# Transposed squares ordered by target quadrant, and diagonal chunk pairs computed on and above the diagonal only

## The chip, the core and the metric

The kernel runs on one core of a Trainium2 chip. Its metric is the device time of one execution in microseconds (us). The kernel before takes 1891.2 us, the median of three runs (1889.86 to 1892.12). The profiled execution took 1890.13 us, of which the profile covers a span of 1888.3 us.

A core has a matrix engine (TensorE, PE in the profile; its loads of stationary weights are PEld), a vector engine (VectorE, DVE), an engine for activation functions (ScalarE, ACT), a general engine (GpSimd, POOL) and a queue that here does nothing but issue transfers (SyncE, SP). Every engine runs its own instructions in the order in which the built program holds them.

## The reference, cut to what matters

The input has four images. Layer 0 turns each into a matrix `q` of 128 channels by 4096 positions and lets its 4096 positions attend to each other:

```python
q = xs.reshape(B, C * R * R, hw)                 # here C*R*R = 128 rows, hw = 4096
energy = jnp.einsum('bci,bcj->bij', q, q)        # 4096 x 4096, symmetric
d = jnp.sqrt(jnp.diagonal(energy, axis1=1, axis2=2))
energy = energy / (d[:, :, None] * d[:, None, :])
attn = jax.nn.softmax(energy, axis=-1)
out = jnp.einsum('bcj,bij->bci', q, attn)
out = gamma * out + xs
```

Layer 1 takes each image as 4096 tokens of 128 features (32 blocks of 128 rows in the kernel), normalises them, adds a linear attention, and then a mixture of eight experts of which the two likeliest are used for each token.

What matters here is that the normalised energy is symmetric, so exp(energy) is too. A square of exp(energy) above the diagonal serves twice: as it is, and transposed.

## The kernel before

The 4096 positions are eight chunks of 512 columns (`NCH = 8`, `CH = 512`), each of four blocks of 128 (`NJ = 4`). For each image, `attend` walks over chunk pairs (i, jc) with jc <= i: 36 pairs, 28 of them with jc < i (off the diagonal), 8 with jc = i (on it). One pair has four steps, one for each 128-row block j. A step computes a 128x512 strip of energy (`pe`), its exponential (`pr`), and the product of the strip with the values, summed up in `po` for chunk i.

```python
for i in range(NCH):
    po = ps_o.tile([P, CH], F32, tag="po", ...)
    def values(pend, i=i, po=po):
        pr, t = pend
        nc.tensor.matmul(po, qT[t // NJ][:, t % NJ, :], pr, start=(t == 0), stop=(t == NJ * (i + 1) - 1))
    for jc in range(i + 1):
        off = jc < i
        if off:
            F = fpool.tile([P, CH // S, NJ, S], F32, tag="F", ...)          # S = 32, fpool: 2 buffers
        for j in range(NJ):
            t = NJ * jc + j
            pe = ps_e.tile([P, CH], F32, tag="pe", ...)                     # 2 buffers
            nc.tensor.matmul(pe, qn[jc][:, ts(j, P)], qn[i], start=True, stop=True)
            pr = ppool.tile([P, CH], F32, tag="pr", ...)                    # 6 buffers
            nc.scalar.activation(pr, pe, AF.Exp, accum_out=sums[:, t, i : i + 1])
            if pend is not None:
                values(pend)
            if off:
                nc.vector.transpose(F[:, :, j, :], pr)                      # 32x32 blocks
            pend = (pr, t)
            ...                                # one step of an older pair's transposed share, if it is due
        if off:
            G = gpool.tile([P, NJ, 4, P], F32, tag="G", ...)                # 3 buffers
            blocks = F.rearrange("p (ib q) j c -> p q ib (j c)", q=4)
            for a in range(4):
                for q in range(4):
                    nc.sync.dma_start(G[ts(q, S), :, a, :], blocks[ts(a, S), q])
            late.append((clock[0] + LAG, transposed_share(b, st, i, jc, G)))
    values(pend)
    o = opool.tile([P, CH], F32, tag="o", ...)
    nc.vector.tensor_copy(o, po)
```

VectorE's transpose works within blocks of 32x32. To make a whole transpose of a square, the blocks must also move between groups of 32 partitions; that is what the 16 transfers from `F` to `G` do, one for each pair of source and target group. The transposed square is then used a little later, four matmuls and four row sums for each pair:

```python
def transposed_share(b, st, i, jc, G):
    pg = ps_g.tile([P, CH], F32, tag="pg", ...)                             # 1 buffer
    for ib in range(NJ):
        nc.tensor.matmul(pg, st["qT"][i][:, ib, :], G[:, ib].rearrange("p a j -> p (a j)"),
                         start=(ib == 0), stop=(ib == NJ - 1))
        junk = work.tile([P, CH], BF16, tag="junk", ...)
        nc.scalar.activation(junk, G[:, ib]..., AF.Copy, accum_out=st["sums"][:, NJ * i + ib, jc : jc + 1])
        if ib == NJ - 1:
            o = st["o"][jc]...
            nc.vector.tensor_tensor(o, o, pg..., ALU.add)
        yield ...
```

Beside the steps of `attend`, two other streams of work are woven in. `prep` loads a part of the next image and makes `qT` (the values) and `qn` (the normalised columns):

```python
def prep(b, kc, st):
    load_tokens(xx, b, 8 * kc, 8)                       # transfers issued by SyncE
    for g in range(2):
        pt = psum_t(f"ptq_{b}_{kc}_{g}")                # TensorE transposes, 2 buffers in all for psum_t
        ...
        nc.vector.tensor_copy(qT..., pt...)
    for s in range(2):
        nc.vector.tensor_tensor(sq, qT[:, s], qT[:, s], ALU.mult)
        nc.vector.tensor_reduce(ss[:, ts(s, NJ)], sq, AX.X, ALU.add)
    pow_neg_half(rn[:, :, 0], ss)                       # GpSimd
    for s in range(2):
        nc.vector.tensor_tensor(qs, qT[:, s], rn..., ALU.mult)
        pt = psum_t(f"ptn_{b}_{kc}_{s}")                # TensorE transposes
        ...
        nc.scalar.activation(qn, pt, AF.Copy)
```

And `layer1` does layer 1 of the image before. In it, `pat` is the attention's matmul, then row statistics on VectorE (`bs_f`, `dm_f`), a power on GpSimd (`rsf`), a normalisation on ScalarE (`xg`), transposes on TensorE (`ptf`), and the experts' matmuls (`py`, with `pbe` for their bias after a transpose `ptg` of the gates). After the last image `layer1` runs alone: this is the tail. The order of instructions on every engine is fixed when the kernel is built; it need not be the order of the source.

Of the kernel before, what the change touches and what calls it, by code (L numbers as in the profile page):

```python
# [9 lines left out]
F32 = mybir.dt.float32  # L10
BF16 = mybir.dt.bfloat16
AF = mybir.ActivationFunctionType
ALU = mybir.AluOpType
# [5 lines left out]
def kernel(  # L19
# [10 lines left out]
    expert_b: bass.AP,  # L30
    out: bass.AP,
):

# [18 lines left out]
    nc = tc.nc  # L54
    P = 128
    B, C, H, W = x.shape
    N = (H // 2) * (W // 2)
    NB = N // P
    CH = 512
    NCH = N // CH  # L60
    NJ = CH // P
    HW2 = W // 2
    KT = 32
    S = 32
# [10 lines left out]
    fpool = ctx.enter_context(tc.tile_pool(name="fpool", bufs=2))  # L75
    gpool = ctx.enter_context(tc.tile_pool(name="gpool", bufs=3))
    work = ctx.enter_context(tc.tile_pool(name="work", bufs=2))
    stat = ctx.enter_context(tc.tile_pool(name="stat", bufs=2))
# [123 lines left out]

    def transposed_share(b, st, i, jc, G):

        pg = ps_g.tile([P, CH], F32, tag="pg", name=f"pg_{b}_{i}_{jc}")
        for ib in range(NJ):
            nc.tensor.matmul(  # L207
                pg, st["qT"][i][:, ib, :], G[:, ib].rearrange("p a j -> p (a j)"),
                start=(ib == 0), stop=(ib == NJ - 1),
            )  # L210
            junk = work.tile([P, CH], BF16, tag="junk", name=f"junk_{b}_{i}_{jc}_{ib}")
            nc.scalar.activation(  # L212
                junk, G[:, ib].rearrange("p a j -> p (a j)"), AF.Copy,
                accum_out=st["sums"][:, NJ * i + ib, jc : jc + 1],
            )
            if ib == NJ - 1:
                o = st["o"][jc].rearrange("p (j a c) -> p a j c", a=4, c=S)
                nc.vector.tensor_tensor(o, o, pg.rearrange("p (a j c) -> p a j c", a=4, c=S), ALU.add)  # L218
            yield "done" if ib == NJ - 1 else None

    def attend(b, st):

        qT, qn = st.setdefault("qT", {}), st.setdefault("qn", {})
        st["sums"] = sums = stat.tile([P, NB, NCH], F32, tag="sums", name=f"sums_{b}")
        st["o"] = []

        for i in range(NCH):
            po = ps_o.tile([P, CH], F32, tag="po", name=f"po_{b}_{i}")
            pend = None

            def values(pend, i=i, po=po):
                pr, t = pend
                nc.tensor.matmul(po, qT[t // NJ][:, t % NJ, :], pr, start=(t == 0), stop=(t == NJ * (i + 1) - 1))  # L233

            for jc in range(i + 1):
                off = jc < i
                if off:
                    F = fpool.tile([P, CH // S, NJ, S], F32, tag="F", name=f"F_{b}_{i}_{jc}")
                for j in range(NJ):
                    t = NJ * jc + j  # L240
                    pe = ps_e.tile([P, CH], F32, tag="pe", name=f"pe_{b}_{i}_{t}")
                    nc.tensor.matmul(pe, qn[jc][:, ts(j, P)], qn[i], start=True, stop=True)  # L242
                    pr = ppool.tile([P, CH], F32, tag="pr", name=f"pr_{b}_{i}_{t}")
                    nc.scalar.activation(pr, pe, AF.Exp, accum_out=sums[:, t, i : i + 1])  # L244
                    if pend is not None:
                        values(pend)
                    if off:
                        nc.vector.transpose(F[:, :, j, :], pr)  # L248
                    pend = (pr, t)
                    clock[0] += 1  # L250
                    if late and late[0][0] <= clock[0]:
                        if next(late[0][1], "done") == "done":
                            late.pop(0)
                    yield
                if off:
                    G = gpool.tile([P, NJ, 4, P], F32, tag="G", name=f"G_{b}_{i}_{jc}")
                    blocks = F.rearrange("p (ib q) j c -> p q ib (j c)", q=4)
                    for a in range(4):
                        for q in range(4):
                            nc.sync.dma_start(G[ts(q, S), :, a, :], blocks[ts(a, S), q])  # L260
                    late.append((clock[0] + LAG, transposed_share(b, st, i, jc, G)))
            values(pend)
            o = opool.tile([P, CH], F32, tag="o", name=f"o_{b}_{i}")
            nc.vector.tensor_copy(o, po)
            st["o"].append(o)
# [7 lines left out]
    def layer1(b, st, alone):  # L273
# [79 lines left out]
        def transpose_rows(g):  # L353
# [3 lines left out]
            if alone:  # L357
                if g % 4 == 0:
                    keep["G"] = gpool.tile([P, 4, 4, P], F32, tag="G", name=f"xnT_{b}_{g}")
                xnT = keep["G"][:, g % 4].rearrange("p j t -> p (j t)")  # L360
# [198 lines left out]
    for b in range(B):  # L559
        streams = []  # L560
        if b == 0:
            for kc, begin, end in ((1, 0, 8), (2, 10, 26), (3, 30, 60)):
                streams.append((prep(0, kc, states[0]), begin, end, 9))
            streams.append((setup_weights(), 60, 70, 3))
        else:
            p = states[b - 1]
            work_left = layer1(b - 1, p, False)
            streams.append((work_left, 9, 138, SIDE))
        if b + 1 < B:
            for kc, at in enumerate((96, 121, 128, 134)):  # L570
                streams.append((prep(b + 1, kc, states[b + 1]), at, at + 9, 9))
        done = [0] * len(streams)
        for t, _ in enumerate(attend(b, states[b])):
            for n, (steps, begin, end, count) in enumerate(streams):
                while t >= begin and done[n] * (end - begin) < (t + 1 - begin) * count:
                    next(steps, None)
                    done[n] += 1
        for steps, *_ in streams:
            for _ in steps:
                pass  # L580
    finish_late()
    last = states[B - 1]
# [40 lines left out]
```

## Time and profile before

| | before |
|---|---|
| time, median of three | 1891.2 us |
| span of the profile | 1888.3 us |
| TensorE busy | 1815.8 us (96%), 5090 matmuls |
| VectorE busy | 900.1 us (48%) |
| ScalarE busy | 957.7 us (51%) |
| GpSimd busy | 292.6 us (15%) |
| `F` to `G` transfers | 1792 of 64 KB, median 2.0 us from issue to landing |
| transfer engines busy with the SyncE queue's packets | 32.4% |

A matmul on 32-bit data is two instructions in the profile, each with a weight load; a TensorE transpose is one. The mean duration of a matmul in the list of groups (595 ns for 512 columns) holds the way through the array, which overlaps with the next one; the distance from one start to the next is shorter and is read from the chain of work in order of time. Idle time of an engine is listed with what ended it. Where the list says "issue", nothing that the profile shows was waited for.

The tail begins about 1743 us after the start of the span.

### The profile page before, as it was taken

What the parts mean: (1) busy time and instruction counts of PE and PEld (TensorE: products, weight loads), DVE (VectorE), ACT (ScalarE), POOL (GpSimd) and SP (SyncE); (2) the same over time, 40 slices, a digit from 0 to 9 for tenths busy, and PEclk for the clock granted to TensorE, in tenths of its full rate; (3) what the DMA queues carried; (4) which work ended last, traced back from release to release, by engine and by line L of the source; (5) the groups of instructions that cost most, each with busy time, mean ns of one, the idle gap of its engine ahead of it and who ended that gap; (6) DMA issues with size and microseconds to landing.
All of it is one profiled execution on the core that took longest, in us unless ns stands there. A gap on an engine that the chain in (4) does not pass through costs nothing.

```text
span 1888.3 us, 20141 instructions
## 1 busy us (share of the span) xinstructions
PE 1815.8 (96%) x5090; PEld 872.5 (46%) x5090; DVE 900.1 (48%) x2201; ACT 957.7 (51%) x2925; POOL 292.6 (15%) x275
## 2 busy tenths in 40 slices
PE   6999999999999999999999999999999999999588
PEld 3444444444554444444554444444455444444543
DVE  3343223345355454555455445563535544443676
ACT  2444444344556545554556545554545645544364
POOL 0000000003000121211200112221300022121336
PEclk9999999999999999999999999999999999999789
DMA  5333343431243233334233333333323323235001
GB/s 118 77 89 74 84 101 85 111 81 46 69 104 78 62 82 75 87 93 96 59 87 76 81 72 84 74 85 85 76 64 90 80 60 85 65 85 117 1 12 34
DMA packets 314274, 145.61 MB, mean 77 GB/s; under 512 B 32528, under 2 KB 314160, under 8 KB 314160
## 3 DMA queue, kind: packets, MB, share of 16 engines
q1 hardware_dynamic: 310528, 142.73, 32.4%
q10 hardware_dynamic: 3632, 1.60, 0.4%
q8 instruction: 42, 0.69, 0.2%
q14 instruction: 72, 0.59, 0.1%
HBM read 18.38 MB, written 8.39 MB: 14 GB/s over the span
## 4 chain that ended last, share of the span: by engine, by line
PE 87%; DVE 5%; POOL 3%; ACT 2%; SPq 1%; DMA 1%; issue 1%; ACTq 0%; POOLq 0%; DVEq 0%
PE po L233 24%; PE pe L242 24%; PE pg L207 20%; PE py L525 6%; PE py L532 5%; DVE df L342 1%; PE pbe L515 1%; PE pat L423 1%; SPq L260 1%; PE ptn L193 1%; POOL T L350 1%; ACT xn L325 1%; PE pgram L368 1%; POOL rsa L109 1%; PE ptx L356 1%; PE ptq L171 1%
## 5 line engine op out<-in xcount | busy, mean ns | idle before, releaser
L244 ACT ACTIVATE pr<-pe 128x512 f32<-128x512 f32 x576 | 343.9, 597 | 580.5 <-PE pe L242 580.1
L233 PE MATMUL po<-pr,qT 128*128 128x512 f32 x1152 | 590.3, 595 | 4.3 <-ACT pr L244 2.7
L248 DVE STREAM_TRANSPOSE F<-pr 128x512 f32<-128x512 f32 x448 | 311.4, 705 | 341.6 <-ACT pr L244 311.6
L242 PE MATMUL pe<-qn,qn 128*128 128x512 f32 x896 | 455.8, 593 | 0.2
L207 PE MATMUL pg<-G,qT 128*128 128x512 f32 x896 | 426.4, 598 | 2.8 <-DMA G<-F 2.8
L233 PEld LDWEIGHTS po<-pr,qT 128*128 128x128 f32 x1152 | 213.9, 190 | 272.1 <-issue 233.0
L212 ACT ACTIVATE junk<-G 128x512 bf16<-128x512 f32 x448 | 276.0, 623 | 4.9 <-DMA G<-F 4.9
L207 PEld LDWEIGHTS pg<-G,qT 128*128 128x128 f32 x896 | 171.0, 192 | 215.3 <-issue 209.3
L242 PEld LDWEIGHTS pe<-qn,qn 128*128 128x128 f32 x896 | 161.4, 190 | 161.1 <-issue 159.7
L534 ACT ACTIVATE tmp<-py,gate 128x128 f32<-128x128 f32 x512 | 145.7, 370 | 172.6 <-PE py L532 163.8
L527 DVE SCALAR_TENSOR_TENSOR acc<-py,gate,acc 128x128 f32<-128x128 f32 x512 | 174.9, 348 | 101.6 <-PE py L525 87.9
L218 DVE TENSOR_TENSOR o<-o,pg 128x512 f32<-128x512 f32 x112 | 76.8, 686 | 230.2 <-PE pg L207 228.9
L538 POOL TENSOR_TENSOR tmp<-tmp 128x512 f32<-128x512 f32 x64 | 81.3, 1271 | 559.2 <-ACT tmp L534 535.7
L532 PE MATMUL py<-ew_sb,xn 128*128 128x512 f32 x256 | 131.9, 601 | 4.1 <-ACT tmp L534 4.1
L242 PE MATMUL pe<-qn 128*128 128x512 f32 x256 | 131.0, 595 | 0.0
L525 PE MATMUL py<-ew_sb,xn 128*128 128x512 f32 x256 | 129.3, 592 | 0.0
L244 ACT ACTIVATION_READ_ACCUMULATOR pr<-pe 128x1 f32 x576 | 114.5, 199 | 0.0
L109 POOL TENSOR_TENSOR rn<-ss,neg_half 128x8 f32<-128x8 f32 x16 | 26.3, 1642 | 433.2 <-DVE ss L183 433.2
L212 ACT ACTIVATION_READ_ACCUMULATOR junk<-G 128x1 f32 x448 | 87.3, 195 | 0.0
L109 POOL TENSOR_TENSOR rsf<-dm_f,neg_half 128x8 f32<-128x8 f32 x16 | 26.3, 1644 | 359.2 <-DVE dm_f L320 359.2
L532 PEld LDWEIGHTS py<-ew_sb,xn 128*128 128x128 f32 x256 | 48.5, 192 | 65.1 <-issue 48.0
L525 PEld LDWEIGHTS py<-ew_sb,xn 128*128 128x128 f32 x256 | 48.0, 190 | 59.2 <-issue 39.4
(114 smaller groups left out, 1221.8 us busy)
## 6 DMA issues: line engine op xcount, KB each, us to landing
G<-F SPq DMA_DIRECT2D x1792, 64.0 KB, 2.0
xx<-in_x_dram SPq DMA_DIRECT2D x64, 128.0 KB, 3.0
T<-in_x_dram SPq DMA_DIRECT2D x16, 512.0 KB, 5.7
out_dram<-acc SPq DMA_DIRECT2D x128, 64.0 KB, 1.8
ew_sb<-in_L_ffn_expert_w_dram ACTq DMA_DIRECT2D x1, 512.0 KB, 5.5
raw_w<-in_L_attn_Wv_dram ACTq DMA_DIRECT2D x1, 512.0 KB
raw_w<-in_L_attn_Wk_dram ACTq DMA_DIRECT2D x1, 256.0 KB
raw_w<-in_L_attn_Wq_dram ACTq DMA_DIRECT2D x1, 256.0 KB
```

The lines of the kernel that those rows point to most:

```text
L207: nc.tensor.matmul(pg, st["qT"][i][:, ib, :], G[:, ib].rearrange("p a j -> p (a j)"), start=(ib == 0), stop=(ib == NJ - 1),)
L212: nc.scalar.activation(junk, G[:, ib].rearrange("p a j -> p (a j)"), AF.Copy, accum_out=st["sums"][:, NJ * i + ib, jc : jc + 1],)
L218: nc.vector.tensor_tensor(o, o, pg.rearrange("p (a j c) -> p a j c", a=4, c=S), ALU.add)
L233: nc.tensor.matmul(po, qT[t // NJ][:, t % NJ, :], pr, start=(t == 0), stop=(t == NJ * (i + 1) - 1))
L242: nc.tensor.matmul(pe, qn[jc][:, ts(j, P)], qn[i], start=True, stop=True)
L244: nc.scalar.activation(pr, pe, AF.Exp, accum_out=sums[:, t, i : i + 1])
L248: nc.vector.transpose(F[:, :, j, :], pr)
L525: nc.tensor.matmul(py, xn[:, k, :], ew_sb[:, 0:4, :], start=True, stop=True)
L527: nc.vector.scalar_tensor_tensor(acc[:, j, :], py[:, ts(e, D)], gate[:, k, e : e + 1], acc[:, j, :], ALU.mult, ALU.add)
L532: nc.tensor.matmul(py, xn[:, k, :], ew_sb[:, 4:8, :], start=True, stop=True)
L534: nc.scalar.activation(tmp[:, jk, e, :], py[:, ts(e, D)], AF.Copy, scale=gate[:, k, 4 + e : 5 + e])
L538: nc.gpsimd.tensor_tensor(tmp[:, :, 0:2], tmp[:, :, 0:2], tmp[:, :, 2:4], ALU.add)
```

## The change

The change has two parts.

**The order within the transposed squares.** `F` and `G` get their quadrant as the outer dimension, so that each of the 16 transfers of a pair reads one run of 2 KB in each partition and writes one such run, instead of four runs of 512 bytes. The number of transfers for a pair and their bytes stay. The readers of `G` (the `pg` matmul and the row sum) then take four runs of 128 columns, 2 KB apart, where they took 512 columns in a row.

**The diagonal pairs.** A pair with jc = i is symmetric itself. Step j now computes only the columns from block j on (512, 384, 256 and 128 columns for `pe`, the exponential and `po`). What lies below the diagonal comes from the transposed share, which a diagonal pair now has too: three transposes, two clears of the part of `F` that is sent but not computed, 16 transfers of 48 KB, three `pg` matmuls and three row sums (384, 256 and 128 columns), and one addition. The last diagonal pair of the last image stays whole, so 31 of 32 pairs change. The row sums get one more column.

The diff, cut to its core:

```diff
     def transposed_share(b, st, i, jc, G):
         pg = ps_g.tile([P, CH], F32, tag="pg", name=f"pg_{b}_{i}_{jc}")
-        for ib in range(NJ):
-            nc.tensor.matmul(
-                pg, st["qT"][i][:, ib, :], G[:, ib].rearrange("p a j -> p (a j)"),
-                start=(ib == 0), stop=(ib == NJ - 1),
+        pgv = pg.rearrange("p (a f) -> p a f", a=4)
+        blocks = [(ib, P) for ib in range(NJ)] if jc < i else [(ib, S * ib) for ib in range(NJ - 1, 0, -1)]
+        for n, (ib, w) in enumerate(blocks):
+            last = n == len(blocks) - 1
+            src = G[:, :, ib, :w]
+            nc.tensor.matmul(pgv[:, :, :w], st["qT"][i][:, ib, :], src, start=(n == 0), stop=last)
             ... (the row sum and the addition follow in the same way)
-        st["sums"] = sums = stat.tile([P, NB, NCH], F32, tag="sums", name=f"sums_{b}")
+        st["sums"] = sums = stat.tile([P, NB, NCH + 1], F32, tag="sums", name=f"sums_{b}")
+        nc.gpsimd.memset(sums[:, :, NCH:], 0.0)
             ...
-                nc.tensor.matmul(po, qT[t // NJ][:, t % NJ, :], pr, start=(t == 0), stop=(t == NJ * (i + 1) - 1))
+                pr, t, c0 = pend
+                nc.tensor.matmul(
+                    po[:, c0:], qT[t // NJ][:, t % NJ, :], pr[:, c0:], start=(t == 0), stop=(t == NJ * (i + 1) - 1)
+                )
             for jc in range(i + 1):
-                off = jc < i
-                if off:
-                    F = fpool.tile([P, CH // S, NJ, S], F32, tag="F", name=f"F_{b}_{i}_{jc}")
+                within = jc == i
+                full = within and b == B - 1 and i == NCH - 1
+                if not full:
+                    F = fpool.tile([P, 4, NJ, NJ, S], F32, tag="F", name=f"F_{b}_{i}_{jc}")
+                    Fb = F.rearrange("p q ib j c -> p ib q j c")
                 for j in range(NJ):
-                    nc.tensor.matmul(pe, qn[jc][:, ts(j, P)], qn[i], start=True, stop=True)
+                    c0 = P * j if within and not full else 0
+                    nc.tensor.matmul(pe[:, c0:], qn[jc][:, ts(j, P)], qn[i][:, c0:], start=True, stop=True)
-                    nc.scalar.activation(pr, pe, AF.Exp, accum_out=sums[:, t, i : i + 1])
+                    nc.scalar.activation(pr[:, c0:], pe[:, c0:], AF.Exp, accum_out=sums[:, t, i : i + 1])
-                    if off:
-                        nc.vector.transpose(F[:, :, j, :], pr)
+                    if not within:
+                        nc.vector.transpose(Fb[:, :, :, j, :], pr)
+                    elif not full and j < NJ - 1:
+                        c1 = max(c0, P)
+                        nc.vector.transpose(Fb[:, c1 // P :, :, j, :], pr[:, c1:])
             ...
-                    G = gpool.tile([P, NJ, 4, P], F32, tag="G", name=f"G_{b}_{i}_{jc}")
-                    blocks = F.rearrange("p (ib q) j c -> p q ib (j c)", q=4)
+                    G = gpool.tile([P, 4, NJ, P], F32, tag="G", name=f"G_{b}_{i}_{jc}")
+                    ib0 = 0
+                    if within:
+                        nc.gpsimd.memset(F[:, :, 1, 2:, :], 0.0)
+                        nc.gpsimd.memset(F[:, :, 2:, 3, :], 0.0)
+                        ib0 = 1
+                    blocks = F.rearrange("p q ib j c -> p q (ib j c)")[:, :, P * ib0 :]
+                    land = G.rearrange("p a ib f -> p a (ib f)")[:, :, P * ib0 :]
                     for a in range(4):
                         for q in range(4):
-                            nc.sync.dma_start(G[ts(q, S), :, a, :], blocks[ts(a, S), q])
+                            nc.sync.dma_start(land[ts(q, S), a, :], blocks[ts(a, S), q, :])
```

More of the change, by code (lines that the diff above doesn't have):

```diff
@@ L205, in transposed_share @@
         pg = ps_g.tile([P, CH], F32, tag="pg", name=f"pg_{b}_{i}_{jc}")
-        for ib in range(NJ):
-            nc.tensor.matmul(
-                pg, st["qT"][i][:, ib, :], G[:, ib].rearrange("p a j -> p (a j)"),
-                start=(ib == 0), stop=(ib == NJ - 1),
-            )
[L211 to L219, printed above, removed]
+        pgv = pg.rearrange("p (a f) -> p a f", a=4)
[4 more added lines that the diff above has]
+            nc.tensor.matmul(pgv[:, :, :w], st["qT"][i][:, ib, :], src, start=(n == 0), stop=last)
+            junk = work.tile([P, 4, P], BF16, tag="junk", name=f"junk_{b}_{i}_{jc}_{ib}")
+            col = jc if jc < i else NCH
+            nc.scalar.activation(
+                junk[:, :, :w], src, AF.Copy, accum_out=st["sums"][:, NJ * i + ib, col : col + 1]
+            )
+            if last:
+                nj = blocks[0][1] // S
+                o = st["o"][jc].rearrange("p (j a c) -> p a j c", a=4, c=S)[:, :, :nj]
+                add = pg.rearrange("p (a j c) -> p a j c", a=4, c=S)[:, :, :nj]
+                nc.vector.tensor_tensor(o, o, add, ALU.add)
+            yield "done" if last else None
     def attend(b, st):
         qT, qn = st.setdefault("qT", {}), st.setdefault("qn", {})
-        st["sums"] = sums = stat.tile([P, NB, NCH], F32, tag="sums", name=f"sums_{b}")
+        st["sums"] = sums = stat.tile([P, NB, NCH + 1], F32, tag="sums", name=f"sums_{b}")
+        nc.gpsimd.memset(sums[:, :, NCH:], 0.0)
         st["o"] = []
@@ L231, in values @@
             def values(pend, i=i, po=po):
-                pr, t = pend
-                nc.tensor.matmul(po, qT[t // NJ][:, t % NJ, :], pr, start=(t == 0), stop=(t == NJ * (i + 1) - 1))
+                pr, t, c0 = pend
+                nc.tensor.matmul(
+                    po[:, c0:], qT[t // NJ][:, t % NJ, :], pr[:, c0:], start=(t == 0), stop=(t == NJ * (i + 1) - 1)
+                )
             for jc in range(i + 1):
-                off = jc < i
-                if off:
-                    F = fpool.tile([P, CH // S, NJ, S], F32, tag="F", name=f"F_{b}_{i}_{jc}")
+                within = jc == i
[3 more added lines that the diff above has]
+                    Fb = F.rearrange("p q ib j c -> p ib q j c")
                 for j in range(NJ):
                     t = NJ * jc + j
+                    c0 = P * j if within and not full else 0
                     pe = ps_e.tile([P, CH], F32, tag="pe", name=f"pe_{b}_{i}_{t}")
-                    nc.tensor.matmul(pe, qn[jc][:, ts(j, P)], qn[i], start=True, stop=True)
+                    nc.tensor.matmul(pe[:, c0:], qn[jc][:, ts(j, P)], qn[i][:, c0:], start=True, stop=True)
                     pr = ppool.tile([P, CH], F32, tag="pr", name=f"pr_{b}_{i}_{t}")
-                    nc.scalar.activation(pr, pe, AF.Exp, accum_out=sums[:, t, i : i + 1])
+                    nc.scalar.activation(pr[:, c0:], pe[:, c0:], AF.Exp, accum_out=sums[:, t, i : i + 1])
                     if pend is not None:
                         values(pend)
-                    if off:
-                        nc.vector.transpose(F[:, :, j, :], pr)
-                    pend = (pr, t)
+                    if not within:
[3 more added lines that the diff above has]
+                        nc.vector.transpose(Fb[:, c1 // P :, :, j, :], pr[:, c1:])
+                    pend = (pr, t, c0)
                     clock[0] += 1
@@ L254, in attend @@
                     yield
-                if off:
-                    G = gpool.tile([P, NJ, 4, P], F32, tag="G", name=f"G_{b}_{i}_{jc}")
-                    blocks = F.rearrange("p (ib q) j c -> p q ib (j c)", q=4)
+                if not full:
+                    G = gpool.tile([P, 4, NJ, P], F32, tag="G", name=f"G_{b}_{i}_{jc}")
[6 more added lines that the diff above has]
+                    land = G.rearrange("p a ib f -> p a (ib f)")[:, :, P * ib0 :]
                     for a in range(4):
                         for q in range(4):
-                            nc.sync.dma_start(G[ts(q, S), :, a, :], blocks[ts(a, S), q])
+                            nc.sync.dma_start(land[ts(q, S), a, :], blocks[ts(a, S), q, :])
                     late.append((clock[0] + LAG, transposed_share(b, st, i, jc, G)))
```

## The prediction, made before the changed kernel was run

> **What bounds the kernel now.** I read the page's busy times and the chain of work that ended last first, then the groups, then the chain in order of time, which gives the distance between starts.
>
> ```profile
> PE 1815.8 (96%) x5090; PEld 872.5 (46%) x5090; DVE 900.1 (48%) x2201; ACT 957.7 (51%) x2925; POOL 292.6 (15%) x275
> ...
> PE 87%; DVE 5%; POOL 3%; ACT 2%; SPq 1%; DMA 1%; issue 1%; ACTq 0%; POOLq 0%; DVEq 0%
> PE po L233 24%; PE pe L242 24%; PE pg L207 20%; PE py L525 6%; PE py L532 5%; DVE df L342 1%; PE pbe L515 1%; PE pat L423 1%; SPq L260 1%; PE ptn L193 1%; POOL T L350 1%; ACT xn L325 1%; PE pgram L368 1%; POOL rsa L109 1%; PE ptx L356 1%; PE ptq L171 1%
> ```
>
> TensorE carries 87% of the chain, 68% in `po`, `pe` and `pg`; no other engine is half full in a way that counts. The chain in order of time gives what an instruction costs (start, length, what):
>
> ```profile
> 984.99 2.15 PE pg L207 x5
> 987.13 0.86 PE pe L242 x2
> ...
> 1003.90 0.74 PE pat L423 x6
> ```
> ```profile
> 926.61 1.78 PE pgram L368 x16
> ```
>
> So 512 columns take 0.429 us, 144 columns 0.123 us, 128 columns 0.111 us. This is 1.2 columns per ns with a floor near 0.11.
>
> The second place that is nearly full is SyncE's queue. The timeline of SP shows 32 transfers in 22.16 us, thus 0.64 to 0.69 us for each; the view of the line gives 599 ns for one issue, to which some 44 ns between issues come.
>
> ```profile
> 990.77 22.16 SPq L260 DMA_DIRECT2D G<-F  x32
> ```
> ```profile
> L260 SPq DMA_DIRECT2D G<-F x1792: 585/599/1900, 37.9 to 1736.2; - x200
> ```
> ```profile
> L545 SPq DMA_DIRECT2D out_dram<-acc x128: 315/438/891, 638.2 to 1885.5; - x128
> ```
>
> A pair's 16 transfers take 16 x 0.643 = 10.3 us, as long as the pair's 12 matmuls (24 x 0.429 = 10.3). Only the diagonal pairs, which send nothing, give the queue air. The output's transfers, of the same bytes but with one side in one run, take 438 ns.
>
> Last, what an idle stretch costs. In the timeline of TensorE (start, length, what, idle before it) eight `ptq` are followed by work for 3.4 us, and then `ptn` waits:
>
> ```profile
> 347.80 1.11 PE L171 MATMUL ptq<-ident,xx 128*128 128x128 f32 x8
> ...
> 351.32 1.02 PE L242 MATMUL pe<-qn,qn 128*128 128x512 f32 x2
> 355.29 1.69 PE L193 MATMUL ptn<-ident,qs 128*128 128x128 f32 x8 [2.96 <-DVE qs L190]
> 356.78 4.79 PE L207 MATMUL pg<-G,qT 128*128 128x512 f32 x8
> ```
>
> From the end of `ptq` (348.9) to `ptn` (355.3) are 6.4 us: a copy (0.7), two squares and two sums on VectorE (2.8), the power on GpSimd (1.64), a product (0.7), and the handing over. And the eight `pg` after it take 4.79 us where such eight take 3.60 elsewhere: the clock fell. With the slowed `ptn` this gap cost some 1.5 us more than its own length.
>
> **What the Trainium skill says.** "TensorE: Matmul & The Clock Gate", LDWEIGHTS, gives columns / 1.2 ns for a weight load, 107 ns for 128; the trace agrees, as the 16 `pgram` at 111 ns are as near to that as to their columns. The same page, What's actually happening, has the clock halve after about an idle window of 3.4 us; the trace agrees in kind (after the gap of 2.96 us weight loads start at 357.63 and 358.49, 0.86 us apart instead of 0.43). "Perfetto Trace Analysis", What "DMA-bound" means, names an issuing sequencer whose track is solid as a bound of its own, with large descriptors as the remedy; the solid stretch of 22 us agrees, the remedy no trace shows yet. "DMA: Bandwidth & Descriptors", Why small descriptors are slow, says that transfers within SBUF do not suffer from small ones; the trace before cannot tell.
>
> **The change part by part.**
>
> *TensorE's work.* A diagonal pair before: 8 matmuls of 512 columns, 16 x 0.429 = 6.86 us. After: `pe` and `po` each 2 x (0.429 + 0.322 + 0.215 + 0.112) = 2.16, and `pg` 2 x (0.322 + 0.215 + 0.112) = 1.30, together 5.61 us. The gain is 1.25 us a pair, **38.7 us** for 31. All of it lies on the path. The reordering of `G` should not touch the `pg` matmuls: their runs are 128 columns long.
>
> *VectorE, ScalarE, GpSimd.* VectorE gets 93 transposes of 256 or 384 columns at 0.4 to 0.55 us (from 0.71 for 512) and 31 additions: some 61 us. ScalarE loses 768 columns of exponential a pair, 0.58 us (slope of 0.75 ns a column, from 308 ns at 128 and 597 at 512), and gets three row sums with their read-outs, 1.9 us: 40 us more. GpSimd gets 62 clears under 0.3 us. They go to 51%, 53% and 16%, beside TensorE.
>
> *SyncE.* 31 x 16 = 496 more transfers, 2288 instead of 1792. If the 2 KB form costs what the output's does (0.44 + 0.04), a pair takes 7.7 us and the queue drains. If it stays at 0.643, image 0 needs 36 x 10.3 = 371 us of issue against some 350 us of TensorE.
>
> *The order on TensorE, which moves.* Set side by side, the orders in which the two built kernels hold TensorE's instructions show something that the diff does not: work has moved out from between some instructions that wait for each other. I added the durations above for what stands between such pairs:
>
> - `ptq` to `ptn`, which needs 6.4 us. Before, the work between is 6.9 us or more except in four places: 5.1, 3.4, 5.1, 5.1; that gives waits of 1.3, 3.0, 1.3, 1.3, and the trace has 1.5, 3.1, 1.2, 1.4. After it is, in order, 6.2, 15.4, 4.3 (image 0), then 2.2, 3.4, 2.2, 5.2, then twice 1.7, 5.1, 4.5, 5.2. The missing time is 0.2 + 2.1 + 12.6 + 9.1 + 9.1 = 33.1 us, **26 us more** than the 6.9 of before.
> - last `pat` to the seventh `ptf` group: 19.8 us or more before, 3.5 us after, in three images. The way through row statistics, power and normalisation takes about 6 us in the trace (529.4 to 535): 2.5 x 3 = **7.5 us**.
> - `ptg` to `pbe`: 3.3 us more; buffers of `py`, `pg` and the shared transposes: about 3 us.
> - Five gaps of 3 us or over at 1.5 us of clock each, against one before: 6 us.
>
> *The tail.* Before, `pg` waits 2.78 us for the last transfer, and the clock falls after it:
>
> ```profile
> 1738.34 5.27 PE L207 MATMUL pg<-G,qT 128*128 128x512 f32 x8 [2.78 <-DMA G<-F]
> ```
>
> After, the last `pg` stands 15.4 us behind its strip instead of 12.0, enough for 1.7 + 10.3 + 2: 4.5 us less.
>
> Sum: -38.7 + 26 + 7.5 + 6.3 + 6 - 4.5 = +3. Some of these waits overlap (a gap for one chain covers another), and a faster queue brings layer 1's `T` earlier, whose lateness belongs to 14 us of gaps at `pgram`. I take 8 us off: about **1886 us**.
>
> **The rivals.** *The work saved is the whole story* (1850 us): if the waits above were covered, 1891.2 - 38.7 - 3. For it speaks that TensorE is the bound at 96%; against it the four waits that the sums reproduce. *SyncE becomes the bound* (1895 to 1910 us): issue stays at 0.64 us, image 0 runs at the queue's pace and loses some 10 to 20 us more. For it speaks that 10.3 us a pair are used up already; against it that the simpler form should be cheaper, and that `pg` now stands 24 to 46 us behind its strip in nearly all pairs (16 to 28 in most before), so a late square is not missed soon. *Crowding on VectorE and ScalarE* (up to 1900 us): the new transposes and sums come in the short diagonal steps at an image's start, where layer 1 begins with a chain over VectorE, GpSimd and ScalarE; 53% of mean load speaks against more than a few us.
>
> **Range and chances.** The middle is 1886 us, the range 1858 to 1908: its low end has the prep waits at half of their sum, its high end has them whole with a slow queue. A gain over 2% (under 1853) needs nearly all waits covered, 0.11; a loss over 2% (over 1929) needs a bound that I don't see, 0.06; the rest, 0.83.
>
> **What would show it.** TensorE's `pe`, `po` and `pg` together shorter by 38 us: the first part. Idle time of `ptn` behind `qs` near 30 us, in gaps of 1 to 5 us in all images: the order. Gaps at the seventh `ptf` group near 2.5 us. Issue of `G` at 0.44 or at 0.60 us decides on the queue; `pg` waiting for `G` or VectorE for `F` by tens of us would make it the bound. The prediction is wrong if `ptn`'s idle time stays under 10 us, or if `pg` at runs 2 KB apart takes more than 0.43 us.

## The result and the profile after

The changed kernel takes **1984.0 us** (median of four runs, 1979.95 to 1988.17), against 1890.5 us for the kernel before in the same session: a ratio of 1.0495, 95% interval 1.0471 to 1.0518. It is 5% slower. The prediction was 1886 us, with 1908 as the high end of its range.

The same two parts of the page as before, busy times and the chain that ended last:

```profile
PE 1823.3 (92%) x5276; PEld 910.7 (46%) x5276; DVE 923.0 (47%) x2325; ACT 967.6 (49%) x3111; POOL 309.2 (16%) x341
...
PE 60%; SPq 19%; DVE 8%; DMA 4%; POOL 3%; issue 3%; ACT 2%; ACTq 0%; POOLq 0%; DVEq 0%
SPq L281 19%; PE pg L214 15%; PE po L240 15%; PE pe L254 15%; PE py L546 5%; PE py L553 5%; DMA G<-F 3%; DVE F L260 2%; DMA T<-in_x_dram 1%; PE pbe L536 1%; PE pgram L389 1%; POOL rn L110 1%; PE ptn L194 1%; SPq L156 1%; POOL rsa L110 1%
```

SyncE's share of the chain went from 1% to 19%, nearly all of it on line 281, the issue of the transfers from `F` to `G`. TensorE is busy for 7.5 us longer although it has 38.7 us less to do. Over the span of 1978.2 us (before: 1888.3) the difference of 89.9 us is 82.4 us of TensorE's idle time (154.9 us instead of 72.5) and these 7.5 us. Since the work fell by 38.7, some 46 us of the busy time are loss. The lower clock accounts for the larger part: the granted clock was halved in 133 us of the span, before in 48; TensorE was busy in 89 and 31 us of these, and half of the 58 between is 29 us. Most of the rest, by estimate some 16 us, is the last matmul before a gap: it counts as busy for its whole way through the array (595 ns for 512 columns, against 429 from start to start), although no other follows. There are 84 gaps over 0.15 us, where there were 32.

By stages, from the first `pe` of an image to that of the next, for image 3 to its last `pe`, where the tail begins in this table (us; the share of SyncE counts the 44 ns after each issue as issuing):

| | image 0 | 1 | 2 | 3 | tail |
|---|---|---|---|---|---|
| before: length | 363.8 | 462.9 | 448.0 | 435.6 | 158.1 |
| after: length | 379.0 | 476.4 | 478.3 | 456.6 | 168.4 |
| TensorE idle, before / after | 6.5 / 22.2 | 5.1 / 24.7 | 2.3 / 26.6 | 2.3 / 19.4 | 40.0 / 46.2 |
| clock halved, before / after | 3 / 17 | 3 / 24 | 0 / 27 | 0 / 21 | 41 / 44 |
| SyncE issuing, share, before / after | .81 / .96 | .72 / .83 | .71 / .84 | .71 / .85 | |

Every stage lost, and with it went the queue. The view of SyncE's lines, for `G` and for the output (count, ns of one issue as minimum/median/maximum, first and last start):

```profile
L281 SPq DMA_DIRECT2D G<-F x2288: 507/589/3374, 26.3 to 1824.5; - x191
```
```profile
L566 SPq DMA_DIRECT2D out_dram<-acc x128: 315/446/581, 668.4 to 1975.3; - x128
```

589 ns, where it was 599: one run of 2 KB in a partition instead of four of 512 bytes saves 10 ns. With the 44 ns between two issues a transfer holds the queue for 0.633 us, and 2288 of them for 1448 us instead of 1152. SyncE's own timeline shows the consequence, first of the kernel before, then of the one after (start, length, what):

```profile
120.12 146.46 SPq L260 DMA_DIRECT2D G<-F  x192
```
```profile
101.16 181.78 SPq L281 DMA_DIRECT2D G<-F  x272
...
871.41 42.81 SPq L281 DMA_DIRECT2D G<-F  x64
914.27 4.91 SPq L156 DMA_DIRECT2D T<-in_x_dram  x4
919.33 90.68 SPq L281 DMA_DIRECT2D G<-F  x118
```

Before, 192 transfers took 0.763 us each: the queue had pauses in it. After, 272 follow each other at 0.668. The longest stretch of issues without a pause of 1.2 us or more is 278 us long; before it was 57 us. Soon after the start of image 2 (874.9) the four loads of `T`, layer 1's tokens, stand in the same line, with 64 transfers (four squares) directly ahead of them. What TensorE then waits for (in all us, times, longest); `pbd` spreads the inverse row sums over the partitions, VectorE multiplies the attention's output by them into `df`, GpSimd adds `df` to `T`, ScalarE normalises `T` into `xn`, and `pgram` is the product of `xn` with itself:

```profile
PE ptn L194 <- DVE qs L191: 31.6, 15, 6.3
PE pbd L359 <- DVE df L363: 27.7, 9, 6.8
PE pgram L389 <- ACT xn L346: 19.2, 5, 5.4
PE pg L214 <- DMA G<-F: 9.7, 4, 7.1
...
PE ptf L463 <- ACT xg L346: 8.3, 9, 3.0
PE ptf L463 <- ACT xn L464: 6.5, 3, 2.2
```

The three longest of these in the kernel before:

```profile
PE pgram L368 <- ACT xn L325: 13.6, 6, 5.4
PE ptn L193 <- DVE qs L190: 12.9, 5, 6.3
...
PE pbd L338 <- DVE df L342: 6.6, 3, 5.5
```

The six sum to 103.0 us; before, the same waits came to 12.9 + 6.6 + 13.6 + 2.8 + 4.4 = 40.3, the last one did not occur. So they hold 62.7 of the 82.4 us of added idle time. Only 9.7 us name the transfers themselves; the rest name VectorE and ScalarE, which wait in their turn. VectorE's waits, first before and then after:

```profile
DVE F L248 <- DMA G<-F: 19.4, 15, 2.6
```
```profile
DVE F L260 <- DMA G<-F: 102.0, 23, 7.3
```

VectorE stands 23 times before a transpose because the two buffers of `F` are not yet sent. All that it does for `prep` and layer 1 comes behind that.

How `T` gets late is seen in the timelines of GpSimd, VectorE and TensorE, further on from the lines of SyncE above. `T` is issued from 914.3 on, and a transfer of it lands 9.1 us later by the median (5.7 before, where the loads went two by two); the last one is issued at 916.9 and lands at 927.0. GpSimd adds `df` to `T` at 927.3. VectorE stands before the row statistics of `T` (`bs_a`) until 929.6, and the next `df` stands behind these. So `pbd`, whose buffer `df` reads, comes 18 us after its last group (914.7). The view puts the first two waits down to `G<-F`, but what is worked on there is `T`, and its landing at 927.0 fits:

```profile
927.26 4.64 POOL L371 TENSOR_TENSOR T<-T,df 128x1024 f32<-128x1024 f32 x2 [21.28 <-DMA G<-F]
```
```profile
929.64 1.65 DVE L332 BATCH_NORM_STATS2 bs_a<-T 128x6 f32<-128x128 f32 x8 [7.59 <-DMA G<-F]
```
```profile
914.71 0.60 PE L359 MATMUL pbd<-ident,rd 128*128 128x128 f32 x4
932.90 1.09 PE L359 MATMUL pbd<-ident,rd 128*128 128x128 f32 x4 [6.21 <-DVE df L363]
```

The second group of four takes 1.09 us instead of 0.60: after the idle 6.21 us the clock is halved. The same is seen where a `ptn` waits; the eight `pg` after it take 4.39 us where eight take 3.60 in an undisturbed stretch of the same timeline:

```profile
390.99 1.94 PE L194 MATMUL ptn<-ident,qs 128*128 128x128 f32 x8 [4.23 <-DVE qs L191]
392.72 4.39 PE L214 MATMUL pg<-G,qT 128*128 128x512 f32 x8
```

### The profile page after: what moved, and what is told of

Same layout as the page of the kernel before. It is cut to its first block, busy times and chain, and to the rows that moved or that the text cites. A ratio compares the mean times of both kernels' runs of the same rounds, so it can differ in the third digit from the quotient of the medians.

```text
span 1978.2 us, 22051 instructions
## 1 busy us (share of the span) xinstructions
PE 1823.3 (92%) x5276; PEld 910.7 (46%) x5276; DVE 923.0 (47%) x2325; ACT 967.6 (49%) x3111; POOL 309.2 (16%) x341
## 4 chain that ended last, share of the span: by engine, by line
PE 60%; SPq 19%; DVE 8%; DMA 4%; POOL 3%; issue 3%; ACT 2%; ACTq 0%; POOLq 0%; DVEq 0%
SPq L281 19%; PE pg L214 15%; PE po L240 15%; PE pe L254 15%; PE py L546 5%; PE py L553 5%; DMA G<-F 3%; DVE F L260 2%; DMA T<-in_x_dram 1%; PE pbe L536 1%; PE pgram L389 1%; POOL rn L110 1%; PE ptn L194 1%; SPq L156 1%; POOL rsa L110 1%
## 5 line engine op out<-in xcount | busy, mean ns | idle before, releaser
L256 ACT ACTIVATE pr<-pe 128x512 f32<-128x512 f32 (+1 forms) x576 | 322.0, 560 | 541.1 <-PE pe L254 484.5
L240 PE MATMUL po<-pr,qT 128*128 128x512 f32 (+3 forms) x1152 | 549.6, 561 | 5.9 <-DVE o L285 2.7
L214 PE MATMUL pg<-G,qT 128*128 128x512 f32 (+2 forms) x1082 | 465.9, 574 | 15.7 <-DMA G<-F 9.7
L217 ACT ACTIVATE junk<-G 128x512 bf16<-128x512 f32 (+3 forms) x541 | 313.1, 587 | 50.8 <-DMA G<-F 48.4
L260 DVE STREAM_TRANSPOSE F<-pr 128x512 f32<-128x512 f32 x448 | 281.1, 681 | 111.8 <-DMA G<-F 102.0
L214 PEld LDWEIGHTS pg<-G,qT 128*128 128x128 f32 x1082 | 209.2, 197 | 251.1 <-issue 235.3
L224 DVE TENSOR_TENSOR o<-o,pg 128x512 f32<-128x512 f32 (+1 forms) x143 | 93.8, 656 | 313.9 <-PE pg L214 313.6
L553 PE MATMUL py<-ew_sb,xn 128*128 128x512 f32 x256 | 134.4, 612 | 10.3 <-DVE acc L548 5.9
L254 PE MATMUL pe<-qn 128*128 128x512 f32 (+3 forms) x256 | 91.8, 442 | 0.0
L346 ACT ACTIVATE xn<-T,nba,rsa 128x128 f32<-128x128 f32 x128 | 51.5, 482 | 71.3 <-DVE nba L343 45.9
L553 PEld LDWEIGHTS py<-ew_sb,xn 128*128 128x128 f32 x256 | 47.8, 195 | 66.2 <-issue 34.3
```

Of the source, the lines that this page charges most:

```text
L214: nc.tensor.matmul(pgv[:, :, :w], st["qT"][i][:, ib, :], src, start=(n == 0), stop=last)
L217: nc.scalar.activation(junk[:, :, :w], src, AF.Copy, accum_out=st["sums"][:, NJ * i + ib, col : col + 1])
L224: nc.vector.tensor_tensor(o, o, add, ALU.add)
L240: nc.tensor.matmul(po[:, c0:], qT[t // NJ][:, t % NJ, :], pr[:, c0:], start=(t == 0), stop=(t == NJ * (i + 1) - 1))
L254: nc.tensor.matmul(pe[:, c0:], qn[jc][:, ts(j, P)], qn[i][:, c0:], start=True, stop=True)
L256: nc.scalar.activation(pr[:, c0:], pe[:, c0:], AF.Exp, accum_out=sums[:, t, i : i + 1])
```

## The experiments

The theory after the result was that the rate at which SyncE issues is the bound, and that the 496 added transfers overrun it. Its rivals: the new layout makes `pg` or the row sums slower; the short diagonal steps crowd VectorE and ScalarE; the added bytes load the transfer engines; the order in which the engines' instructions were built is worse for a reason of its own. All times are medians, with the ratio to the kernel before and its 95% interval.

| run | what | us | ratio |
|---|---|---|---|
| after | the change | 1984.0 | 1.0495 (1.0471 to 1.0518) |
| e1 | layout alone | 1889.6 | 0.9994 (0.9986 to 1.0003) |
| e2 | diagonal pairs alone | 1991.4 | 1.0532 (1.0516 to 1.0548) |
| e3 | before, with 496 transfers nobody reads | 2015.2 | 1.0662 (1.0646 to 1.0678) |
| e4 | after, without the diagonal transfers | 1868.8 | 0.9881 (0.9865 to 0.9898) |
| e5 | after, `T` loaded by GpSimd | 1964.8 | 1.0390 (1.0375 to 1.0406) |
| e6 | after, `T` and `xx` loaded by GpSimd | 1923.2 | 1.0171 (1.0156 to 1.0186) |
| e7 | after, 4 of 16 transfers as copies on GpSimd | 1853.3 | 0.9802 (0.9787 to 0.9816) |
| e8 | after, diagonal transfers issued by GpSimd | 1867.9 | 0.9882 (0.9866 to 0.9899) |
| e9 | before, 4 of 16 transfers as copies | 1884.5 | 0.9968 (0.9955 to 0.9980) |
| e10 | e7, `T` loaded by GpSimd | 1869.2 | 0.9887 (0.9872 to 0.9902) |

**e1, the layout alone.** All diagonal pairs stay whole:

```diff
-                full = within and b == B - 1 and i == NCH - 1
+                full = within
```

> The 2 KB layout alone, with whole diagonal pairs as before; TensorE's order is that of before. Queue theory (SyncE's issue, some 0.63 us a transfer, is the bound that the 496 added transfers overrun): the load is that of before, so 1885 to 1892 us, and an issue costs 589 ns. Layout theory (matmuls and row sums that read G in runs 2 KB apart, or transposes that write F with one more dimension, are slower): clearly over 1900 us, and pg over 0.43 us apart or F over 711 ns. Narrow-step theory (the short diagonal steps leave the chains at an image's start uncovered): 1890 us as well.

Measured: no difference from before. An issue takes 589 ns, the idle times of the stages are those of before within 1 us. One `pg` follows another in 429 ns and a row sum takes 618 ns, both as before. So neither minds runs 2 KB apart, and the layout, made to relieve the queue, brings it 10 ns of 643.

**e2, the diagonal pairs alone**, with `F` and `G` laid out as before (four runs of 512 bytes); the lines that carry this:

```diff
-    F = fpool.tile([P, 4, NJ, NJ, S], F32, tag="F", ...)
-    G = gpool.tile([P, 4, NJ, P], F32, tag="G", ...)
-    nc.sync.dma_start(land[ts(q, S), a, :], blocks[ts(a, S), q, :])
+    F = fpool.tile([P, CH // S, NJ, S], F32, tag="F", ...)
+    G = gpool.tile([P, NJ, 4, P], F32, tag="G", ...)
+    nc.sync.dma_start(G[ts(q, S), ib0:, a, :], blocks[ts(a, S), q])
```

> The diagonal part alone, with runs of 512 bytes as before. TensorE's built order is that of the changed kernel. Queue theory: the issue costs 599 instead of 589 ns, so as slow as the changed kernel or a little slower, 1984 to 2005 us. Layout theory: 1890 us or less. If the 2 KB runs mattered for the transfers themselves (128 packets each instead of 32): over 2010 us.

Measured: 1991.4 us, the whole loss of the change and 7 us more, though the intervals of the two ratios just overlap. If the 7 us are real, they fit a full queue, to which the 10 ns an issue are worth something: 2288 of them are 23 us of its time.

**e3, transfers that nobody reads**, in the kernel before; no other work is added:

```diff
+                elif not (b == B - 1 and i == NCH - 1):
+                    spare = gpool.tile([P, 4, NJ * P], F32, tag="G", ...)
+                    for a in range(4):
+                        for q in range(4):
+                            nc.sync.dma_start(spare[ts(q, S), a, : 3 * P], qn[i][ts(a, S), : 3 * P])
```

> The kernel before, with 16 transfers of 48 KB for each of 31 diagonal pairs added whose target nobody reads; all matmuls, exponentials and transposes stay as before. Queue theory: the whole loss appears without any narrow step, 1890 plus some 80 to 120 us, 1970 to 2010. Narrow-step theory: hidden, 1890 to 1905 us.

Measured: 2015.2 us, 5 us above the range that the queue theory gave, from 1890.9 beside it. The transfers alone cost 124 us; less the 38.7 us of TensorE's work that the change saves and this kernel doesn't, 1976 us, close to the 1984 of the change. The crowding theory falls: here are no short steps and no added work on VectorE or ScalarE. The same waits come up as in the profile after (the waits of TensorE):

```profile
PE pgram L373 <- ACT xn L330: 32.9, 8, 5.4
PE ptn L193 <- DVE qs L190: 22.7, 13, 6.3
PE pbd L343 <- DVE df L347: 15.1, 7, 7.3
```

The spare tiles also take `G` buffers, so that this run doesn't part the queue from the buffers; e8 does.

**e4, the change without its transfers.** `G` of a diagonal pair is cleared by GpSimd instead of filled. This leaves the share below the diagonal out of the result; the matmuls, row sums and additions on it stay.

```diff
+                    if within:
+                        nc.gpsimd.memset(land, 0.0)
+                    else:
                         ... (the 16 transfers)
```

> The changed kernel without the 496 transfers of the diagonal pairs; their G is filled with zeros by GpSimd instead, so the share from below the diagonal within diagonal pairs is left out of the output. All matmuls, row sums and transposes of the changed kernel stay. Queue theory: the queue is back at its load of before, 1848 to 1868 us. Narrow-step theory: still 1950 to 1985 us.

Measured: 1868.8 us, 115 us under the change, with everything of it there but the transfers. It lies 0.8 us above what was expected. Image 0, with 365.8 us and a clock that was halved for 17 us, gained nothing on before: there `ptn` still waits 4.2, 2.0 and 4.2 us, as in the change (4.2, 2.9 and 4.2).

**e8, the same transfers from another engine.** Bytes, buffers and work are those of the change; the 496 diagonal transfers are issued by GpSimd. Their packets do not stay, other than the expectation says: by the pages' counts each has 48 on SyncE's queue, and 32 on the queue that GpSimd's transfers go to.

```diff
+                    issuer = nc.gpsimd if within else nc.sync
-                            nc.sync.dma_start(land[ts(q, S), a, :], blocks[ts(a, S), q, :])
+                            issuer.dma_start(land[ts(q, S), a, :], blocks[ts(a, S), q, :])
```

> The changed kernel with the 496 transfers of the diagonal pairs issued by GpSimd instead of SyncE; nothing is left out, and the transfers, their bytes and their packets stay. Queue theory (issue, not data): 1850 to 1872 us. Theory that the transfers' data crowd the transfer engines: still over 1950 us.

Measured: 1867.9 us, as without the transfers. 116 us depend on who issues them, none can be seen on what they carry. The buffers as a cause fall, and so do the transfer engines, which are busy with these queues for 36.6% of the shorter time, where it was 35.0% in the change:

```profile
q1 hardware_dynamic: 162304, 167.15, 35.0%
```
```profile
q1 hardware_dynamic: 138496, 142.73, 31.4%
q0 software_dynamic: 15872, 24.41, 5.2%
```

(the change, then e8: packets, MB, share). Nor do transfers pile up behind the issue in the change: from issue to landing they take 2.0 us by the median in both runs. One thing moved along: in the built order `ptn` stands uncovered in fewer places (after the start it waits 2 times, 2.8 us in all; in the change 14 times, 25.3 us). So the 116 us are those of the full queue together with those of the order that comes with it. The page's busy line, and the view of the issuing line, SyncE and GpSimd:

```profile
PE 1782.7 (96%) x5276; PEld 896.9 (48%) x5276; DVE 948.9 (51%) x2325; ACT 973.2 (52%) x3111; POOL 554.5 (30%) x837
```
```profile
L282 SPq DMA_DIRECT2D G<-F x1792: 507/589/1720, 32.7 to 1712.9; - x200
L282 POOL DMA_DIRECT2D G<-F x496: 496/498/674, 26.5 to 1616.7; - x166
```

TensorE is back at 96%. GpSimd pays 498 ns for each, 247 us in all, and can afford it. The stages give back 20.0, 28.4, 33.2, 20.3 and 11.5 us (images 0 to 3, tail). The Trainium skill ("DMA: Bandwidth & Descriptors", Issuing engines are not separate DMA queues) says that issuing from several engines saves the sequencer's time only, which is usually small beside the transfer. The first agrees with this run. The second was no comfort: 0.63 us of issue stand beside 2.0 us to landing, but in these traces transfers overlap and issues don't.

**e5 and e6, what stands in line behind the squares.** First the loads of `T`, then also those of the next image's parts (`xx`) go to GpSimd; all 2288 transfers of `G` stay on SyncE.

```diff
-                nc.sync.dma_start(dst[p0 : p0 + 32], src[s, r1, :, k0 : k0 + nk, :])
+                nc.gpsimd.dma_start(dst[p0 : p0 + 32], src[s, r1, :, k0 : k0 + nk, :])
```

(e6; in e5 for the call that loads `T` only)

> The changed kernel with the 16 loads of layer 1's T issued by GpSimd instead of waiting in SyncE's queue behind G. The built distances from ptq to ptn are those of the changed kernel. Theory that T comes late because it stands behind G in the queue: pbd waiting for df falls from 27.7 to under 8 us and the low clock after it goes with it, 1945 to 1960 us in all, ptn's idle time stays near 31 us. Theory that these waits come from crowding on VectorE and ScalarE in the short diagonal steps: 1975 to 1985 us.

> As e5_T_gpsimd, and the loads of xx go by GpSimd too. SyncE still issues all 2288 transfers of G. In the built order ptn now stands 6.2 us or more behind ptq everywhere. Theory that the built order costs time by itself: ptn's idle time falls from 31 to under 15 us, another 25 to 35 us less than e5 with the clock, 1915 to 1935 us, and image 0 stays at 375 to 380 us since its G still needs 36 x 10.1 us of issue. Theory that only the live queue counts and waits merely move: within 8 us of e5.

Measured: 1964.8 us, 5 us above the range, and 1923.2 us, within it, but with 369.3 us in image 0 instead of the 375 to 380 expected. In the waits of TensorE e5 removes the lateness of `T` (27.7 to 6.6) and leaves `ptn`'s; e6 removes most of that (6.3 us of it stand at the very start, in the kernel before too). First e5, then e6:

```profile
PE ptn L194 <- DVE qs L191: 31.6, 14, 6.3
...
PE pbd L359 <- DVE df L363: 6.6, 3, 5.5
```
```profile
PE ptn L194 <- DVE qs L191: 12.2, 5, 6.3
```

So, taken away in this order, the 116 us are 19 behind `T`, some 42 behind `xx`, and 55 that remain with the squares: in e6 SyncE still holds 10% of the chain, and image 0 still issues for .95 of its time. Part of the 42 is likely the built order: with the loads elsewhere, TensorE's instructions stand otherwise in the program, with more work between `ptq` and `ptn`. These two can't be parted by these runs, since the order moved along with the load of the queue.

**e7, fewer transfers.** Of the 16 blocks of a square, four keep their group of 32 partitions. GpSimd copies them, 1716 transfers remain.

```diff
                     for a in range(4):
+                        nc.gpsimd.tensor_copy(land[ts(a, S), a, :], blocks[ts(a, S), a, :])
                         for q in range(4):
-                            nc.sync.dma_start(land[ts(q, S), a, :], blocks[ts(a, S), q, :])
+                            if q != a:
+                                nc.sync.dma_start(land[ts(q, S), a, :], blocks[ts(a, S), q, :])
```

> The changed kernel with the four of 16 transfers whose source and target are the same 32 partitions replaced by GpSimd copies: 12 transfers a pair, 1716 in all, fewer than the 1792 of before. Queue theory: the work saved comes through, 1848 to 1868 us. Theory that the diagonal pairs' narrow steps and added work on VectorE and ScalarE cost the time: over 1920 us.

Measured: 1853.3 us, 2% under before, the fastest of all. SyncE issues for .79 of image 0 and .68 of the others, GpSimd is at 35%:

```profile
PE 1775.4 (96%) x5276; PEld 898.1 (48%) x5276; DVE 980.1 (53%) x2325; ACT 973.3 (53%) x3111; POOL 648.4 (35%) x913
```

**e9, the same copies in the kernel before**, to tell the change from the relief:

```diff
                     for a in range(4):
+                        nc.gpsimd.tensor_copy(G[ts(a, S), :, a, :], blocks[ts(a, S), a])
                         for q in range(4):
-                            nc.sync.dma_start(G[ts(q, S), :, a, :], blocks[ts(a, S), q])
+                            if q != a:
+                                nc.sync.dma_start(G[ts(q, S), :, a, :], blocks[ts(a, S), q])
```

> The kernel before, with the four blocks of each square that stay in their group of 32 partitions copied by GpSimd (448 copies of 32x512, taken to cost about 591 ns each) and only the other twelve transferred: 1344 transfers instead of 1792, and nothing of the change. It tells how much of the gain of the changed kernel with such copies is the change itself and how much is a queue with less to do than before. Theory (the change saves TensorE 38.7 us wherever the queue keeps pace): the queue was no bound before, so only the small waits behind it go, ptn's 6.9 and some of the tail's, and in the built order every ptn now stands at 6.9 us or more behind its ptq: 1870 to 1885 us, so that the change is worth 17 to 32 us on top of it. Rival (most of the gain of the copies is the queue's relief and the change itself is worth little): 1850 to 1862 us.

Measured: 1884.5 us, at the edge of what the theory gave. The relief alone is worth 6 us to a kernel whose queue was not the bound, and the change is worth 31 us on top of it (1884.5 to 1853.3), of the 38.7 predicted for its work. TensorE's busy time falls by 1809.9 - 1775.4 = 34.5 us, with 10 us more at half clock, thus by estimate some 5 us lost: together 39.5.

**e10, e7 with `T` loaded by GpSimd:**

```diff
-        load_tokens(T, b, 0, KT)
+        load_tokens(T, b, 0, KT, nc.gpsimd)
```

> The changed kernel with those copies (1716 transfers) and, besides, the tokens of layer 1 (T) loaded by GpSimd. With the copies alone it took 1853 us, pgram waited 20.7 us for xn and ptn 13.1 us. In the built order no ptn now stands less than 6 us behind its ptq, where four stood at 4.9 to 6.2 before. Theory (the queue still holds back what stands behind it): ptn under 8 us, pgram under 17, 1842 to 1850 us. Rival (the queue has room by now, and who issues T no longer matters): 1850 to 1856 us.

Measured: 1869.2 us. Both expectations missed: it is 16 us slower than e7. `pgram`'s wait fell as expected (20.7 to 8.5), `ptn`'s to 10.3 only, but another came up in the waits of TensorE:

```profile
PE po L233 <- ACT pr L244: 14.8, 8, 2.5
```
```profile
PE po L240 <- ACT pr L256: 18.0, 9, 3.0
```

(first e9, then e10; in the kernel before it was 2.7 us, in e7 it is 0.6). In all, TensorE idles 11.0 us more than in e7 (2.2 of them at the start, where `ptq` waits for `xx`) and is busy 6 us longer. Why ScalarE's exponential comes late there is not settled: instructions stand in another order on all engines, and no run takes this apart.

## Why the prediction was wrong

**The step that failed is the queue's.** The prediction set out the fork: 0.44 + 0.04 us if the 2 KB form costs what the output's does, or still 0.643 and then 371 us of issue against 350 of TensorE in image 0. It put its middle on the first branch: its sum has no term for the queue, and takes 8 us off in part for a faster one. The 0.44 was read from transfers to the memory of the chip, and taken over to transfers within the core because both have one simple side. Measured: 0.633. What the prediction cited from the Trainium skill ("Perfetto Trace Analysis", What "DMA-bound" means), large descriptors as the remedy for a full sequencer, didn't hold for this queue: descriptors four times as large saved 1.7% of an issue (e1).

**The rival that was right was too small.** "SyncE becomes the bound" was put at 1895 to 1910 us, for 10 to 20 us in image 0. Image 0 lost 15.2 us, as sized. But the other images lost 13.5, 30.3 and 21.0, and the tail 10.3, which the rival left out. By sums there is room in these images: 36 pairs take some 365 us of issue there, and the images some 450. But the queue serves in order, and what is late is not an average. `T` and `xx` wait behind squares that are not needed yet: in images 1 to 3 a square's last transfer lands some 11 us before `pg` takes it, by the median. A sign that the prediction itself had named did come true: VectorE waits for `F` by tens of us (102.0, from 19.4).

**The clock was mis-sized too**: "five gaps at 1.5 us", 6 us, became some 29. Gaps of 3 us or over went from 7 to 15 in the whole span, and the stretches at half clock from 8 to 18.

**`T` had the wrong sign.** 8 us were taken off, in part since "a faster queue brings layer 1's `T` earlier". The queue was not faster, `pbd` waited 21.1 us more, and e5 gave 19 us back. `pgram`, whose gaps the prediction laid to `T`, hardly changed there (19.2 to 18.8 us).

**`ptn` and `ptf` were right in kind, with something behind them that the prediction didn't see.** 33.1 us were worked out for 14 waits of `ptn`. The 31.6 measured hold 6.3 at the very start, which were there before, so that they stand near 33.1 by luck: the 14 waits took 25.3, twelve of them within 0.4 us of what was worked out and the two of 4.7 only 1.1 each, since a `py` had waited 2.9 us just ahead. The increase was 18.7 us, not 26. For the seventh `ptf` 7.5 were worked out and 8.7 measured (in three images 2.18 us, and 0.62 to 0.77 just after). They were taken as a property of the order, beside the question of the queue. e6, e7 and e8 change nothing but who moves what, and `ptn` waits 12.2, 13.1 and 9.1 us there, the 6.3 of the start included; `ptf`'s added waits are gone in e7 and e8, though not in e6. `pg` stands some 39 us behind the last `pe` of its pair in the images after the first (18 to 19 before; 38 in e6, whose queue still holds all squares; 18 to 19 in e8, 15 in e7). The prediction read this distance as slack; it goes with the load of the queue. That the order was packed around a full queue is the likely reading, but no run holds the order as it is and relieves the queue of the squares.

**TensorE's work was right**: 38.7 us predicted, some 39.5 between e9 and e7. `pg` at runs 2 KB apart cost nothing (e1), and crowding was rightly put aside (e3).

**The tail** was to gain 4.5 us and lost 10.3. The last `pg` stands farther behind its strip, but its transfer was still in the queue. TensorE's timeline, where 2.78 us stood before:

```profile
1826.75 5.94 PE L214 MATMUL pg<-G,qT 128*128 128x512 f32 x8 [7.10 <-DMA G<-F]
```

## What to carry to other kernels

Count an issuing queue like an engine: transfers times the measured time from one issue to the next of that same kind of transfer, stage by stage, and ask what else stands in the same line. When it is nearly full, a change that adds transfers can pay on the waits behind the queue and again in the clock after the longer ones; hand some of the issues, or the blocks that needn't be moved between partitions, to an engine with time to spare. If a built order shows consumers drifting away from their producers, ask whether a full queue drove them apart before counting the distance as slack.

## What the runs showed of the hardware that was not expected

Between parts of the core's own memory, the issue cost is one of the transfer, not of its bytes or its runs: 599 ns with four runs of 512 bytes in each of 32 partitions (e2), 589 with one run of 2 KB or of 1.5 KB (after, and the unread transfers of e3), and no less when a quarter of the transfers is taken away (599 in e9). On the same queue a transfer to the output took 446 ns, a load of `xx` (128 KB) 449 and one of `T` (512 KB) 594 (after). A transfer of 48 KB issued by GpSimd took 498 ns (e8). A GpSimd copy of 32x512 took about as long as an issue, 607 ns by the median in e7, on an engine with time to spare.

TensorE's busy time is not all work: in the changed kernel it grew by 7.5 us while its work fell, through 58 more busy us at half clock and through 52 more gaps, before each of which the last matmul runs out alone.
